# Two graph-attention layers on one core: TensorE in the source's order

## The chip, the cores and the metric

The kernel runs on one core of one Trainium2 chip, as one launch. The metric is the time of that launch in device microseconds. The version before takes 2741.27 us (median of three runs, 2739.28 to 2741.64 us).

A core has five engines with a queue each. In this kernel TensorE (PE) does matrix products and transposes, VectorE (DVE) and ScalarE (ACT) do elementwise work and reductions, GpSimd (POOL) issues the gathers and scatters (indirect DMAs), and SyncE (SP) issues the plain DMAs.

## What is computed

The inputs are `x`, 8 batches of 2048 nodes with 256 features, and `adj`, a 2048 x 2048 adjacency matrix of few ones (some 0.8% of its entries, and the diagonal). There are two layers, and each is followed by a residual and a layernorm over the features:

```python
# layer 0
h1, h2, h3 = x @ W1, x @ W2, x @ W3
e = leaky_relu(h1 @ h2.T, 0.2);  e = where(adj > 0, e, -1e12)
x = layernorm(x + relu(softmax(e) @ h3))
# layer 1, 4 heads of 64
q = x @ W;  e = leaky_relu(e_src[i] + e_dst[j]) where adj > 0   # per head
x = layernorm(x + elu(softmax(e) @ q))
```

Here `e_src` and `e_dst` are the products of `q` with the two halves of the vector `a`, per head. Only the neighbours of a node enter its softmax, so the kernel never forms a full 2048 x 2048 score matrix.

## The kernel before

**Units and slots.** The nodes are sorted by degree and cut into 16 tiles of 128. A tile t has `SLOTS[t]` slots, from 12 to 38, 301 in all: slot k of a tile is, for each of its 128 nodes, the k-th neighbour. A *unit* is one layer, one half of the batch (4 of 8 batches) and one tile. There are 64 units: layer 0 first half, layer 0 second half (both from the tile with 12 slots to the one with 38), then the two halves of layer 1. A unit with 38 slots is done in two parts of 19.

**What one unit of layer 0 does.** `before0` gathers the unit's own rows `xo`, copies them to a residual buffer `xr`, transposes them on TensorE (`transposed`, two stages with a copy by ScalarE after each), and multiplies by A = W1 W2^T (`projected`, two stages) to get `g`. For each slot GpSimd gathers the 128 neighbour rows into a ring of 16 buffers of two slots (`chunk_job`). `logits0` has VectorE form the products of the rows with `g`, four instructions per slot, and then a softmax over the slots. `sums0` has ScalarE scale each slot's rows by their weights, four instructions, and TensorE add the slot to an accumulator in PSUM by a product with an identity (`add_slot`); then the ring buffer is free. `after0` takes the finished sum `hs`: it transposes it, multiplies it by W3, adds the residual on VectorE, normalises on VectorE and ScalarE, stores the row to `x1s`, transposes it again, and makes the rows `q` of layer 1 with their attention terms `so` in four more products. The rows `q` are scattered to a table by GpSimd eight steps later.

**Layer 1.** `logits1` needs one small addition per slot and head, `sums1` multiplies by the weights on VectorE (four chunks of five) or ScalarE (the fifth), and TensorE adds as before. `after1` does the elu, the residual and the layernorm, and scatters the result. For the tile with 38 slots the two parts are combined first (`shares` gives their factors, with small products on TensorE).

**What sets the order.** All of this is written as Python generators, and a driver, `tick` (L928), advances them: one call is a *step*. A step issues gathers while ring buffers are free (`pump`), up to two slots of scores, and up to two `yield`s of the work at the head of each of three queues: `starts` (`before0`, `before1`), `ends` (`after0`, `after1`) and `lists` (the extraction of each tile's neighbours, done with VectorE in the first half of layer 0). Between two steps one slot's sum is issued. A start is queued when half of the unit three places earlier is summed (L961). A unit's sums don't begin while more than one end is still open (L950).

The program order that comes out is binding for GpSimd alone: `tc.manual_schedule(engines={mybir.EngineType.Pool})` (L339). For the other engines a planner reorders the instructions with its own model of their times, and the engines then run their queues in the planned order.

**Buffers.** Four PSUM banks (`ps`) serve transposes and projections in turn and four (`psa`) the accumulators. `g` has two buffers, `xo` two, `xr` three, `wide` four (for `xT`, `hT`, `y`, `x1T`), and `q` one.

Of the kernel before, what the change touches and what calls it, by code (L numbers as in the profile page):

```python
# [38 lines left out]
RING = 16  # L39
LEAD = 5  # L40
LATE = 6

SHARE = 5

# [81 lines left out]
def fast_path(  # L126
# [59 lines left out]
    def wide_tile(name):  # L186
        return wp.tile([P, 2 * QW], F32, tag="t", name=name)
# [148 lines left out]
        nc.vector.tensor_copy(orderR[:, :, r], pr)  # L336
    nc.vector.scalar_tensor_tensor(orderP, orderR, 2.0, half, ALU.mult, ALU.add)
    setup.__exit__(None, None, None)
    ctx.enter_context(tc.manual_schedule(engines={mybir.EngineType.Pool}))  # L339

    def checks():

# [51 lines left out]
    def normalise(dst, y, b, rstd, nmr):  # L394
# [2 lines left out]
            bias=nmr[:, b : b + 1], scale=rstd[:, b : b + 1],  # L397
        )

    def transposed(src, name, dst):  # L400

        for i in range(2):
            pt = ps_tile(f"ps_t_{name}_{i}")
            for j in range(4):
                nc.tensor.transpose(pt[:, ts(j, P)], src[:, ts(4 * i + j, P)], ident)  # L405
            yield
            nc.scalar.copy(dst[:, ts(i, 512)], pt)  # L407
        yield

    def projected(srcT, weight, name, evict):  # L410
        for i in range(2):
            pp = ps_tile(f"ps_p_{name}_{i}")
            for j in range(2):
                for k in range(KC):
                    nc.tensor.matmul(  # L415
                        pp[:, ts(j, C)],
                        lhsT=srcT[:, ts((2 * i + j) * KC + k, P)],
                        rhs=weight[:, k, :],
                        start=(k == 0),
                        stop=(k == KC - 1),  # L420
                    )
            yield
            evict(i, pp)
        yield

    class Unit:
        def __init__(self, layer, h, t):
# [78 lines left out]
    def before0(u):  # L506
        xo = xop.tile([P, HC], F32, tag="xo", name=f"xo_{u.name}")
        gather(xo, xg[u.h][:, :], order[:, u.t : u.t + 1])
        u.xr = xrp.tile([P, 2, HW], F32, tag="xr", name=f"xr_{u.name}")
        for r in range(2):  # L510
            for c in range(2):
                nc.sync.dma_start(
                    u.xr[64 * c : 64 * c + 64, r, :], xo[64 * r : 64 * r + 64, ts(c, HW)]
                )
        for _ in range(4):
            yield
        xT = wide_tile(f"xT_{u.name}")
# [144 lines left out]
    def after0(u):  # L662
        h, t, n = u.h, u.t, u.name
        while evictions:
            evictions.popleft()()
        hs = u.hs
        hT = wide_tile(f"hT_{n}")
        yield from transposed(hs, f"h_{n}", hT)
        y = wide_tile(f"y0_{n}")[:, :HC]

        def residual(i, pp):
            nc.vector.scalar_tensor_tensor(
                y[:, ts(i, 512)], pp, 0.0, u.xr[:, i, :], ALU.max, ALU.add
            )

        yield from projected(hT, w.w3, f"h_{n}", residual)
        yb = y.rearrange("p (b c) -> p b c", b=HB)
        mv = yield from statistics(yb, n)
        yield
        yield  # L680
        rstd, nmr = factors(mv, n)
        yield
        for b in range(HB):
            normalise(yb, yb, b, rstd, nmr)
            if b % 2 == 1:
                yield
        nc.sync.dma_start(x1s[h][ts(t, P), :], y)
        x1T = wide_tile(f"x1T_{n}")
        yield from transposed(y, f"x1_{n}", x1T)
        qrow = qp.tile([P, 2, QW], F32, tag="q", name=f"q_{n}")  # L690
        so = sp.tile([P, 2, HG // 2], F32, tag="so", name=f"so_{n}", bufs=2)
        for i in range(HB):
            r, j = divmod(i, 2)
            pq = ps_tile(f"ps_q_{n}_{i}")
            for k in range(KC):
                nc.tensor.matmul(  # L696
                    pq[:, : C + 2 * H],
                    lhsT=x1T[:, ts(i * KC + k, P)],
                    rhs=w.wqs[:, k, :],
                    start=(k == 0),  # L700
                    stop=(k == KC - 1),
                )
            yield
            nc.scalar.copy(qrow[:, r, ts(j, CD)], pq[:, :CD])
            nc.vector.tensor_copy(so[:, r, ts(j, H)], pq[:, CD : CD + H])  # L705
        for c in range(2):
            nc.sync.dma_start(
                own_d[h][ts(t, P), ts(c, HG // 2)].rearrange("(r p) g -> p r g", r=2),
                so[64 * c : 64 * c + 64],
            )  # L710

        def store():
            for r in range(2):
                scatter(
                    f"q{h}",
                    qg[h].rearrange("n (q c) -> (n q) c", q=2),
                    orderP[:, t, r : r + 1],
                    qrow[:, r, :],
                )
            tabled[0] += 1  # L720

        late.append((clock[0] + 8, store))
# [62 lines left out]
    def sums1(u):  # L785
        u.xr = xrp.tile([P, 2, HW], F32, tag="xr", name=f"xr_{u.name}")
        nc.sync.dma_start(u.xr.rearrange("p r c -> p (r c)"), x1s[u.h][ts(u.t, P), :])
        while evictions:
            evictions.popleft()()
        u.accs = []  # L790
        for i, (k0, K) in enumerate(u.parts):
            while u.p[i] is None:
                yield 0
# [23 lines left out]
            for c in range(chunks):  # L817
# [5 lines left out]
                for s in range(n):  # L823
# [1 line left out]
                    if s == n - 1:  # L825
                        credits[0] += 1
                    yield 1
            u.accs.append(acc)

    def after1(u):  # L830
        h, t, n = u.h, u.t, u.name
        v = u.accs[0]
        if len(u.accs) == 2:
            fs = shares(u, HG)
            v = wide_tile(f"v_{n}")[:, :HC]
            v = [v[:, ts(r, HW)] for r in range(2)]
            v2 = wide_tile(f"v2_{n}")[:, :HC]
            for r in range(2):
                for i, d in ((0, v[r]), (1, v2[:, ts(r, HW)])):
                    nc.vector.tensor_tensor(  # L840
                        d.rearrange("p (a d) -> p a d", d=D),
                        u.accs[i][r].rearrange("p (a d) -> p a d", d=D),
                        fs[:, i, r, :].unsqueeze(2).to_broadcast([P, HG // 2, D]),
                        ALU.mult,
                    )
                nc.vector.tensor_tensor(v[r], v[r], v2[:, ts(r, HW)], ALU.add)
            yield

        ex = wide_tile(f"ex_{n}")[:, :HC]
        for r in range(2):  # L850
# [89 lines left out]

    for t in up[:3]:
# [324 lines left out]
```

## Time and profile before

| | |
|---|---|
| median of the runs | 2741.27 us |
| the profiled execution | 2741.96 us |
| its span, first to last instruction | 2740.1 us |
| TensorE busy, matmuls | 1857.8 us, 68% of the span |
| TensorE busy, weight loads | 792.3 us, 29% |
| VectorE busy | 2270.1 us, 83% |
| ScalarE busy | 1827.9 us, 67% |
| GpSimd busy | 1515.4 us, 55% |
| granted TensorE clock, mean | 0.842 |
| moved by DMA | 749.51 MB, 274 GB/s in the mean |

"Busy" counts the instructions themselves and no waiting; an engine's idle time before an instruction is listed with what ended it. A mean over the span hides that the stages differ: the setup takes until some 200 us, layer 0 until some 1720 us, layer 1 the rest. A score instruction on VectorE takes 424 ns in the mean and its readout 82 ns, a scaling on ScalarE 506 ns from start to end (consecutive ones start 0.4 us apart), a product of a slot's sum 653 ns with eight of them in flight together.

### The profile page before, as it was taken

The page shows a single profiled execution, that of the slowest core. Times are in us where ns is not written, and L with a number is a line of the kernel's source. Part 1 is how long each engine was busy: PE and PEld are TensorE (multiplying, and loading weights), DVE is VectorE, ACT ScalarE, POOL GpSimd, SP SyncE. Part 2 cuts the span into 40 slices and gives each one's busy share as a digit, 9 for nine tenths or more (in the row PEclk, how much of TensorE's full clock was granted, in tenths as well). Part 3 has the DMA queues.
Part 4 walks back from the last instruction along what each step waited for, and adds up shares of the span by engine and source line. Part 5 has one row for each costly group of instructions (what it writes and reads, how often), then busy time and mean ns, then how long its engine had stood idle before and what let it go on. Part 6 is the DMA issues. An engine that isn't in the chain of part 4 may idle for free. (4 is left out here: it accounts for less than half of the span.)

```text
span 2740.1 us, 42566 instructions
## 1 busy us (share of the span) xinstructions
PE 1857.8 (68%) x12003; PEld 792.3 (29%) x12003; DVE 2270.1 (83%) x7247; ACT 1827.9 (67%) x4937; POOL 1515.4 (55%) x1506
## 2 busy tenths in 40 slices
PE   0148888888786866686878767756656667655763
PEld 0124434333332333343434323312221222211221
DVE  7679999999987876777787786788888888888996
ACT  6137787878879986867878779644445555554454
POOL 1353454545444544544454545577767777777773
PEclk9569999999988988898988888877877878877876
DMA  9996776777765566767686774899789998997892
GB/s 388 380 376 207 270 262 245 260 245 263 261 221 200 183 215 215 252 212 268 219 277 217 242 263 154 287 332 357 268 315 354 348 344 317 358 351 269 305 354 89
DMA packets 248036, 749.51 MB, mean 274 GB/s; under 512 B 55712, under 2 KB 73248, under 8 KB 241648
## 3 DMA queue, kind: packets, MB, share of 16 engines
q0 software_dynamic: 192064, 644.32, 66.5%
q1 hardware_dynamic: 54464, 101.21, 10.4%
q8 instruction: 98, 1.61, 0.2%
q10 hardware_dynamic: 1264, 1.18, 0.1%
q14 instruction: 146, 1.20, 0.1%
HBM read 721.50 MB, written 84.48 MB: 294 GB/s over the span
## 5 line engine op out<-in xcount | busy, mean ns | idle before, releaser
L612 PE MATMUL acc<-s,ident 64*64 64x512 f32 x9632 | 1336.4, 653 | 469.0 <-issue 285.4
L543 DVE CUSTOM_DVE_ANT_0 j<-s,g 128x256 bf16<-128x256 f32 x2408 | 1019.9, 424 | 199.1 <-DMA s<-xg,idx 133.0
L191 POOL DMA_INDIRECT s<-xg,idx x602 | 632.4, 1051 | 771.7 <-ACT s L634 280.9
L634 ACT ACTIVATE s<-s,e 128x256 f32<-128x256 f32 x2408 | 1000.1, 506 | 28.3 <-DVE e L569 27.4
L191 POOL DMA_INDIRECT s<-qg,idx x602 | 614.8, 1021 | 233.4 <-issue 123.7
L612 PEld LDWEIGHTS acc<-s,ident 64*64 64x64 f32 x9632 | 391.1, 144 | 1211.5 <-issue 777.6
L813 DVE TENSOR_TENSOR s<-s,p 128x2048 f32<-128x2048 f32 (+1 forms) x262 | 577.5, 2222 | 0.0
L809 ACT ACTIVATE s<-s,e 128x64 f32<-128x64 f32 x1472 | 357.8, 335 | 47.1 <-DVE e L777 35.8
L543 DVE DVE_READ_ACCUMULATOR2_ANT e<- 128x1 f32 x2408 | 197.0, 82 | 0.0
L696 PE MATMUL ps_q<-wqs,x1T 128*128 128x264 f32 x512 | 147.7, 426 | 35.9 <-ACT x1T L407 25.1
L199 POOL DMA_INDIRECT out_dram<-o,oidx x128 | 130.2, 1017 | 71.5 <-ACT o L395 36.7
L405 PE MATMUL ps_t_x<-ident,xo 128*128 128x128 f32 x256 | 56.7, 365 | 162.7 <-DMA xo<-xg,order 162.6
L383 ACT ACTIVATE z<-mv,roots 128x4 f32<-128x4 f32 x64 | 19.0, 297 | 212.2 <-DVE mv L373 212.1
L747 DVE TENSOR_TENSOR e<-s,own 128x32 f32<-128x32 f32 (+1 forms) x312 | 56.9, 186 | 104.0 <-DMA s<-qg,idx 97.6
L415 PE MATMUL ps_p_g<-A,xT 128*128 128x256 f32 x512 | 129.4, 399 | 8.9 <-DVE so L705 5.2
L415 PE MATMUL ps_p_h<-w_sb,hT 128*128 128x256 f32 x512 | 127.8, 392 | 1.4 <-ACT hT L407 1.4
L696 PEld LDWEIGHTS ps_q<-wqs,x1T 128*128 128x128 f32 x512 | 100.8, 206 | 88.4 <-ACT x1T L407 32.8
L395 ACT ACTIVATE o<-xr,nmr,rstd 128x256 f32<-128x256 f32 x128 | 66.3, 589 | 76.9 <-DVE nmr L391 67.3
L415 PEld LDWEIGHTS ps_p_g<-A,xT 128*128 128x128 f32 x512 | 96.7, 196 | 53.2 <-ACT s L634 8.1
L763 ACT ACTIVATE e<-e 128x304 f32<-128x304 f32 (+11 forms) x34 | 14.9, 439 | 143.7 <-DVE e L762 143.7
L491 DVE MAX8 m<-nb 128x8 f32<-128x2048 f32 x44 | 100.5, 2286 | 11.9 <-DMA nb<-edges,order 11.7
L415 PEld LDWEIGHTS ps_p_h<-w_sb,hT 128*128 128x128 f32 x512 | 92.0, 189 | 63.3 <-issue 17.9
(130 smaller groups left out, 1486.2 us busy)
## 6 DMA issues: line engine op xcount, KB each, us to landing
adj<-in_adj_dram SPq DMA_DIRECT2D x16, 1024.0 KB, 8.9
edges<-adj SPq DMA_DIRECT2D x16, 1024.0 KB, 19.8
xr<-xo SPq DMA_DIRECT2D x128, 128.0 KB, 6.9
x1s<-y SPq DMA_DIRECT2D x32, 512.0 KB, 7.3
xr<-x1s SPq DMA_DIRECT2D x32, 512.0 KB, 6.9
s<-xg,idx POOLq DMA_INDIRECT x602
s<-qg,idx POOLq DMA_INDIRECT x602
xg<-in_x_dram SPq DMA_DIRECT2D x4, 2048.0 KB
```

Of the source, the lines that this page charges most:

```text
L191: nc.gpsimd.indirect_dma_start(out=dst, out_offset=None, in_=table, in_offset=AT(ap=index, axis=0), bounds_check=table.shape[0] - 1, oob_i ...
L199: ins = nc.gpsimd.indirect_dma_start(out=table, out_offset=AT(ap=index, axis=0), in_=src, in_offset=None)
L395: nc.scalar.activation(dst[:, b, :], y[:, b, :], AF.Identity, bias=nmr[:, b : b + 1], scale=rstd[:, b : b + 1],)
L415: nc.tensor.matmul(pp[:, ts(j, C)], lhsT=srcT[:, ts((2 * i + j) * KC + k, P)], rhs=weight[:, k, :], start=(k == 0), stop=(k == KC - 1),)
L491: nc.vector.max(m[:, ts(i, 8)], v)
L543: nc.vector.tensor_tensor_reduce(out=jt, in0=rows[:, s, ts(b, C)], in1=u.g[:, ts(b, C)], scale=1.0, scalar=0.0, op0=ALU.mult, op1=ALU.add, ...
L612: nc.tensor.matmul(acc[r][64 * c : 64 * c + 64, :], lhsT=ident[rr, rr], rhs=rows[rr, s, c * 2 * w_ : (c + 1) * 2 * w_].rearrange("p (j w) ...
L634: nc.scalar.activation(v, v, AF.Copy, scale=u.p[i][:, b, k : k + 1])
L696: nc.tensor.matmul(pq[:, : C + 2 * H], lhsT=x1T[:, ts(i * KC + k, P)], rhs=w.wqs[:, k, :], start=(k == 0), stop=(k == KC - 1),)
L747: nc.vector.tensor_tensor(e[:, c * CHUNK : c * CHUNK + ns, :].rearrange("p s (b g) -> p s b g", b=HB), rows[:, :ns, :].rearrange("p s (b w ...
L809: nc.scalar.activation(v[:, a, g, :], v[:, a, g, :], AF.Copy, scale=pv[:, a, g : g + 1])
L813: nc.vector.tensor_tensor(v, v, pv.unsqueeze(3).to_broadcast([P, n * HB, H, D]), ALU.mult)
```

## The change

TensorE is added to the engines that follow the source's order. So that this order is a sensible one, the source is rewritten around it:

- `pause(n)` waits until the driver has made n more steps. `transposed`, `projected` and the `q` products now issue a stage and its copy in the same step and take one step per stage; there are fixed distances of `GAP` = 2 steps after a pair of transposes and before the first ones of an end, of 4 steps before the transposes of the normalised rows, and of 8 steps between the gather of `xo` and its transposes.
- The statistics, their factors and the normalisation of an end follow each other without pauses.
- The driver advances the two oldest ends in each step, and the head alone of `starts` and of `lists`; a unit's sums wait only when more than two ends are open.
- In layer 1 the combination of two parts (`combine`) is put in the queue `evictions`, which is emptied ahead of the next unit's sums, where it stood in `after1`.

The instructions and their number stay the same.

```diff
+GAP = 2
...
-    ctx.enter_context(tc.manual_schedule(engines={mybir.EngineType.Pool}))
+    ctx.enter_context(
+        tc.manual_schedule(engines={mybir.EngineType.Pool, mybir.EngineType.PE})
+    )
...
+    def pause(steps):
+        then = clock[0] + steps
+        while clock[0] < then:
+            yield
+
     def transposed(src, name, dst):
         for i in range(2):
             pt = ps_tile(f"ps_t_{name}_{i}")
             for j in range(4):
                 nc.tensor.transpose(pt[:, ts(j, P)], src[:, ts(4 * i + j, P)], ident)
-            yield
             nc.scalar.copy(dst[:, ts(i, 512)], pt)
-        yield
+            yield from pause(1)
+        yield from pause(GAP)
...
-            yield
             evict(i, pp)
-        yield
+            yield from pause(1)
...
-        for _ in range(4):
-            yield
+        yield from pause(LATE + 2 if u.index else 2)
         xT = wide_tile(f"xT_{u.name}")
...
         hs = u.hs
+        yield from pause(GAP)
         hT = wide_tile(f"hT_{n}")
...
         mv = yield from statistics(yb, n)
-        yield
-        yield
         rstd, nmr = factors(mv, n)
-        yield
         for b in range(HB):
             normalise(yb, yb, b, rstd, nmr)
-            if b % 2 == 1:
-                yield
         nc.sync.dma_start(x1s[h][ts(t, P), :], y)
+        yield from pause(2 * GAP)
         x1T = wide_tile(f"x1T_{n}")
...
-            yield
             nc.scalar.copy(qrow[:, r, ts(j, CD)], pq[:, :CD])
             nc.vector.tensor_copy(so[:, r, ts(j, H)], pq[:, CD : CD + H])
+            yield from pause(1)
...
-            u.accs.append(acc)
-
-    def after1(u):
...
+            accs.append(acc)
+        u.v = accs[0]
+
+        def combine():
             fs = shares(u, HG)
...
+        if len(accs) == 2:
+            evictions.append(combine)
+
+    def after1(u):
+        h, t, n = u.h, u.t, u.name
+        while evictions:
+            evictions.popleft()()
+        v = u.v
...
         for queue in queues:
-            for _ in range(min(len(queue), 2)):
-                if queue and next(queue[0], queue) is queue:
-                    queue.popleft()
+
+            for work in list(queue)[: 2 if queue is ends else 1]:
+                for _ in range(2):
+                    if next(work, work) is work:
+                        queue.remove(work)
+                        break
         clock[0] += 1
...
-        while len(ends) > 1:
+        while len(ends) > 2:
             tick(0)
```

More of the change, by code (lines that the diff above doesn't have):

```diff
@@ L789, in sums1 @@
             evictions.popleft()()
-        u.accs = []
+        accs = []
         for i, (k0, K) in enumerate(u.parts):
@@ L827, in sums1 @@
                     yield 1
-            u.accs.append(acc)
-    def after1(u):
-        h, t, n = u.h, u.t, u.name
-        v = u.accs[0]
-        if len(u.accs) == 2:
+            accs.append(acc)
+        u.v = accs[0]
+        def combine():
             fs = shares(u, HG)
-            v = wide_tile(f"v_{n}")[:, :HC]
-            v = [v[:, ts(r, HW)] for r in range(2)]
-            v2 = wide_tile(f"v2_{n}")[:, :HC]
+            v = wide_tile(f"v_{u.name}")[:, :HC]
+            u.v = [v[:, ts(r, HW)] for r in range(2)]
+            v2 = wide_tile(f"v2_{u.name}")[:, :HC]
             for r in range(2):
-                for i, d in ((0, v[r]), (1, v2[:, ts(r, HW)])):
+                for i, d in ((0, u.v[r]), (1, v2[:, ts(r, HW)])):
                     nc.vector.tensor_tensor(
                         d.rearrange("p (a d) -> p a d", d=D),
-                        u.accs[i][r].rearrange("p (a d) -> p a d", d=D),
+                        accs[i][r].rearrange("p (a d) -> p a d", d=D),
                         fs[:, i, r, :].unsqueeze(2).to_broadcast([P, HG // 2, D]),
@@ L845, in after1 @@
                     )
-                nc.vector.tensor_tensor(v[r], v[r], v2[:, ts(r, HW)], ALU.add)
-            yield
+                nc.vector.tensor_tensor(u.v[r], u.v[r], v2[:, ts(r, HW)], ALU.add)
+        if len(accs) == 2:
[5 more added lines that the diff above has]
+        v = u.v
         ex = wide_tile(f"ex_{n}")[:, :HC]
```

## The prediction

> **What bounds the kernel now.** I read the page's busy shares first, then busy time by stage, then the waits of the longest stage, then one of its units in the timeline. No engine bounds the whole span (VectorE 83%), so I cut it by when a unit's last sum left TensorE (every slot is 8 `acc` matmuls): layer 0's first half of the batch ends at 960 us, its second half at 1719 us, layer 1 fills the rest. Each row: stretch and length; busy time and count on PE, weight load, DVE, ACT, POOL; clock, DMA share, GB/s.
>
> ```profile
> 205.00:505.00 300.00, 254.55 (x1356) 119.72 (x1352) 289.48 (x1149) 234.37 (x573) 138.23 (x133) 0.93 0.71 249
> 505.00:825.00 320.00, 264.77 (x1432) 114.37 (x1432) 302.47 (x1270) 250.28 (x620) 154.86 (x146) 0.92 0.73 246
> 825.00:960.00 135.00, 98.65 (x648) 42.55 (x640) 107.25 (x513) 125.47 (x314) 66.29 (x65) 0.86 0.58 194
> 960.00:1650.00 690.00, 510.58 (x3152) 249.05 (x3148) 522.92 (x2500) 545.55 (x1341) 323.65 (x309) 0.86 0.70 237
> 1720.00:2740.00 1020.00, 629.81 (x4888) 219.61 (x4888) 861.59 (x1368) 526.46 (x1805) 723.17 (x709) 0.80 0.85 309
> ```
>
> VectorE bounds 205 to 825 (96%, 95%); it also extracts the neighbour lists there. ScalarE bounds 825 to 960 (93%). In 960 to 1650 nothing passes 79%: that stage has room. Its waits on TensorE and VectorE (total us, times, longest):
>
> ```profile
> PE ps_t_x L405 <- DMA xo<-xg,order: 122.5, 13, 12.2
> ...
> DVE j L543 <- DMA s<-xg,idx: 112.0, 74, 7.2
> ```
>
> TensorE's 510.6 us of work and 122.5 us of waiting for a unit's own rows make 633 of the 690. One unit shows how (start, length, work, idle before it):
>
> ```profile
> 1103.91 7.10 PE L612 MATMUL acc<-s,ident 64*64 64x512 f32 x64
> 1122.30 1.09 PE L405 MATMUL ps_t_x<-ident,xo 128*128 128x128 f32 x4 [11.29 <-DMA xo<-xg,order]
> ```
> ```profile
> 1113.88 1.04 POOL L191 DMA_INDIRECT xo<-xg,order  x1 [0.30 <-issue]
> ...
> 1125.60 1.09 POOL L191 DMA_INDIRECT s<-xg,idx  x1 [5.12 <-PE acc L612]
> ```
>
> The planner placed the transposes of `xo` behind eight slots done in one burst; `xo` is only requested at 1113.88 and lands 8.4 us later. Meanwhile no sum runs, no ring buffer comes free, GpSimd stops gathering (5.12 us) and VectorE starves.
>
> **What the Trainium skill says.** "TensorE: Matmul & The Clock Gate", § Measured speedup vs the span model: matmuls start and end strictly in program order. The trace agrees: sums whose rows were scaled stand 11.29 us behind one transpose. "DMA: Bandwidth & Descriptors", § Anatomy of one DMA, prices a GpSimd-issued DMA at some 2 us plus bytes at 436 GB/s, 3.2 us for the 512 KB of `xo`; here it took 8.4 us behind other gathers, and that is what I use. "Perfetto Trace Analysis", § Optimization Strategy, advises looking for gaps regime by regime on the engine that binds; done above.
>
> **The change, part by part.** No instruction is added or dropped. TensorE's order becomes the source's, ScalarE, VectorE and SyncE stay with the planner. Positions below are driver steps (calls of `tick`), counted through the generators.
>
> *1. The wait for `xo` (gain).* `xo` is gathered eight steps ahead of its transposes, where it had two; its four `xr` copies on SP stay behind the gather as before. A step in this stage is some 2.3 us, so eight are 18 us against 8.4 us plus two gathers queued ahead (2 x 1.3). The wait goes. Sums come one per step, so buffers and gathers come evenly too. What is late next: ScalarE with 545.6 us, then VectorE with 522.9; TensorE's own work is 510.6. The best share a binding engine reaches here is 93 to 96% (rows above), but with other engines idle for 15% and more. Here VectorE is nearly as full, and ScalarE's queue holds copies of what TensorE makes one instruction earlier. Bounds: 82% (hardly better than now) and 95%. I take 88%: 545.6 / 0.88 = 620, gain 70 us; ends 665 (gain 25) and 574 (gain 116).
>
> *2. Stages spread and two units overlapped (nothing, with a bound).* Projections of a unit go from 10 steps after its end to 21. Work that hides it: the next unit's sums, 12 to 38 steps. VectorE's residual and statistics, ScalarE's normalisation, `x1s<-y` on SP come 5 to 6 steps later; the next reader of `x1s` is layer 1, hundreds of us on. The transposes of `y` have six steps (13 us) after the last projection; in the timeline around 1104 to 1115 that chain took 11. The one `q` buffer is tighter: the scatter goes out 29 steps after a unit's end, the next unit's `q` copies come K + 17 steps after it, 1 to 3 steps for K of 13 to 15, against 7 to 10 before. A landing of 8 us could hold ScalarE up to 5 us in ten units: 0 to 50 us, of which the half beside a fuller VectorE is free. I count it inside the 88%.
>
> *3. The queue of starts (loss).* Only the head of `starts` is driven, at one stage per step: a start takes 8 + 4 + 2 steps and the next begins one step on, so 15 per unit, where it took 5. The first units have 12 to 17 slots, so starts run just in time: g of units 2 to 8 gets its projection after slot 5, 5, 4, 4, 4, 3, 1 of the unit before; from unit 9 on it is early again. In source order TensorE cannot take it sooner. So VectorE, having scored unit n, waits for unit n's first sums before it can score n+1. Gap: weights of the softmax 3.0 us (from 376.1 to 379.1 in the timeline of VectorE), then 6, 6, 5, 5, 5, 4, 2 slots on ScalarE at 4 x 0.41 = 1.65 us, its copies between them some 3.5 us, last sum, projection and copy of g 3.0 us: 19.4, 19.4, 17.7, 17.7, 17.7, 16.1, 12.8, together 121 us. In the gap VectorE still does the lists (two or three MAX8 at 2.29 and one or two replacements at 2.28: 7 to 11 us). Then it scores: 112 slots at 4 x 0.467 = 1.87 us = 209 us, and 2.5 us of other work squeezed between them in each unit = 18 us. Sum 348 us. Counting scores in the timeline, these seven units took from 216.0 to 513.2, 297 us. Loss 51 us. Bounds: the gap 4 us shorter or longer in each unit: 23 to 79. Nothing gives it back: from unit 9 on VectorE is full as before.
>
> *4. `combine` ahead of the next unit's sums (nothing).* It runs for two units of layer 1. The next unit needs the accumulators it frees, before and after; the same 6 multiplications and adds of 0.69 us.
>
> *5. Layer 1.* TensorE has only sums there, in the order of the source already; DMA (85%) and VectorE bind. 0, bounds -8 and +8.
>
> Sum against the profiled run's own 2742.0 us: -70 + 51 + 0, rounded to -20: 2722; the median of the runs is 0.7 us less, so 2721.
>
> **The rivals.**
> *A. Slower: ScalarE's queue keeps waiting for TensorE.* Each unit of layer 0 has 10 copies and 4 q copies out of PSUM; the planner puts them into ScalarE's queue by its own clock. If TensorE is a microsecond behind it at each, ScalarE stays near today's 79 to 82%; the gain of part 1 shrinks to 25 us and part 3 decides: 2741 - 25 + 51 = 2767. The turning point is 545.6 / (690 - 51) = 85%. For it: in 960 to 1650 ScalarE waits already 42.6 us for the softmax and 27.4 us for statistics. Against: copies other than those of `xo` cost it only 26 us.
> *B. Much faster.* The lists and the residuals fill the gap of part 3 (loss 25) and ScalarE reaches 92% (593 us, gain 97): 2669. Against: 7 to 11 us of lists don't fill 17.
> *C. The wait for `xo` hides nothing.* Then the second half stays, 2741 + 51 = 2792. Against: 633 of 690 us.
> *D. No change*: parts 1 and 3 cancel, 2741.
>
> **How the numbers follow.** Forecast 0.44, A 0.32, B 0.10, C 0.05, D 0.09. 0.2% (5.5 us) is about what a measurement of this kernel tells from no change. Faster 0.54, same 0.09, slower 0.37. The forecast's own range is 2695 to 2736; with A and most of B it is 2660 to 2790.
>
> **What would show it.** Right: in the second half no wait of TensorE on `xo`, ScalarE at 88%, last sum of that half's units some 620 us after the first; in 205 to 530 us VectorE's share falls from 96 to about 83%, with waits on the g copy. Wrong: VectorE as full as before at the start (part 3), ScalarE below 85% with waits on PSUM copies or on the q scatter (part 1), or layer 1 different from 1020 us.

## The result, and the profile after

The changed kernel takes **2905.24 us** (median of four runs, 2901.32 to 2906.62) against 2741.45 us for the kernel before, measured beside it: a ratio of 1.059, interval 1.0566 to 1.0613. The forecast was 2721 us, with a range of its own from 2695 to 2736 and of 2660 to 2790 with the rivals. The profiled execution took 2901.32 us (its span is 2899.5 us), so it stands for the median.

The span is cut where a unit's last sum leaves TensorE, which is read from the trace of each kernel by counting `acc` matmuls, eight to a slot (us):

```
                            before    after
to the end of unit 0         205.2    201.4
units 1 to 8                 349.1    497.7   +148.6
units 9 to 15                405.8    398.6     -7.2
units 16 to 30               690.0    663.5    -26.5
unit 31                       68.9     66.7     -2.2
layer 1, first half          509.2    524.9    +15.7
layer 1, second half         483.9    520.1    +36.2
after the last sum            28.0     26.6     -1.4
```

With the 3.8 us gained by the end of unit 0 this adds up to the 159.4 us between the two spans. So three things happened: units 1 to 8 lost far more than the 51 us of part 3, units 16 to 30 gained far less than the 70 us of part 1, and layer 1, which was to stay as it is, lost 52 us. TensorE's granted clock was a little lower than before (0.821 against 0.842 in the mean), but its busy time did not grow (1853.6 us against 1857.8), so the lower clock is not what cost the time.

Busy time of the changed kernel by stage (stretch and length; PE, weight load, DVE, ACT, POOL; clock, DMA share, GB/s), in two answers:

```profile
201.00:699.00 498.00, 279.79 (x1589) 136.24 (x1585) 366.34 (x1421) 273.89 (x669) 163.44 (x157) 0.76 0.54 180
...
1097.00:1761.00 664.00, 528.10 (x3152) 245.35 (x3148) 524.03 (x2484) 538.51 (x1337) 322.30 (x306) 0.90 0.73 245
1828.00:2899.00 1071.00, 635.36 (x4880) 220.23 (x4880) 861.63 (x1366) 526.61 (x1808) 715.56 (x706) 0.80 0.82 293
```
```profile
205.00:530.00 325.00, 166.06 (x944) 80.81 (x944) 223.72 (x861) 165.56 (x406) 96.49 (x93) 0.73 0.50 168
```

VectorE, busy 96% of the first stretch before, is busy 223.72 of 325 us = 69% there now (83% was forecast). In the second half ScalarE is busy 538.51 of 664 us = 81% (88% was forecast, 79% before).

**Units 2 to 8.** From the last score of unit 1 to the last score of unit 8 the trace of the changed kernel has 415.9 us (230.5 to 646.4), where the prediction had 348 and the kernel before 297. Waits of the stretch, weight loads left out (what waits, for what; total us, times, longest):

```profile
PE acc L620 <- ACT s L642: 150.7, 7, 33.3
ACT e L571 <- DVE e L570: 131.6, 7, 30.9
...
DVE so L709 <- ACT q L708: 55.6, 10, 10.9
...
POOL nb L192 <- PE acc L620: 42.7, 2, 24.5
DVE j L551 <- ACT g L531: 36.5, 9, 7.8
```

VectorE, ScalarE and TensorE take turns: TensorE waits for scaled rows seven times, 21.5 us each on average (150.7 / 7), ScalarE as often for the weights. One gap, after unit 5, on VectorE and on GpSimd (start, length, work, idle before it):

```profile
463.22 0.23 DVE L577 TENSOR_TENSOR e<-e,s 128x64 f32<-128x64 f32 x1
474.33 0.16 DVE L709 COPY so<-ps_q 128x4 f32<-128x4 f32 x1 [10.88 <-ACT q L708]
478.47 0.43 DVE L551 CUSTOM_DVE_ANT_0 j<-s,g 128x256 bf16<-128x256 f32 x1 [3.98 <-ACT g L531]
...
479.45 2.30 DVE L500 MAX8 m<-nb 128x8 f32<-128x2048 f32 x1
```
```profile
470.46 0.98 POOL L192 DMA_INDIRECT s<-xg,idx  x1 [20.34 <-ACT s L642]
473.85 0.98 POOL L192 DMA_INDIRECT nb<-edges,order  x1 [2.41 <-ACT s L642]
```

The last score ends at 461.4 and the next starts at 478.47: 17.1 us, against 17.7 for this gap in the prediction. But the lists that were to run in it come after it. The list's gather needs a ring buffer, which the sums of this very gap free, so it goes out at 473.85; and on VectorE the copy of `so`, which waits for ScalarE's copy of `q`, and the first score stand in front. Over the seven gaps (124.5 us by the trace; 121 forecast) VectorE spends 9.1 us on lists. Of the 69.3 us of lists in the stretch, 60.2 run between scores.

**Units 16 to 30.** TensorE's largest waits there:

```profile
PE ps_t_x L415 <- ACT y L398: 50.1, 12, 7.1
PE ps_q L701 <- ACT x1T L416: 23.0, 6, 5.7
```

The wait for `xo` (122.5 us before) is gone; in a unit's timeline a slot's sums now stand between the stages (1200.22 below), where before eight or nine slots came in one burst, 14 times in these units (the longest burst is now six slots):

```profile
1197.28 1.09 PE L620 MATMUL acc<-s,ident 64*64 64x512 f32 x8
1198.30 1.99 PE L425 MATMUL ps_p_g<-A,xT 128*128 128x256 f32 x8
1200.22 1.09 PE L620 MATMUL acc<-s,ident 64*64 64x512 f32 x8
1201.24 1.99 PE L425 MATMUL ps_p_g<-A,xT 128*128 128x256 f32 x8
```

**Layer 1.** One wait grew on GpSimd and one on VectorE, the longest from 15.5 to 19.8 us and from 4.1 to 13.1 us. Layer 1 of the kernel before, then of the changed one:

```profile
POOL out_dram L199 <- ACT o L395: 36.7, 14, 15.5
...
DVE e L747 <- DMA s<-qg,idx: 91.7, 67, 4.1
```
```profile
POOL out_dram L200 <- ACT o L398: 76.9, 31, 19.8
...
DVE e L752 <- DMA s<-qg,idx: 144.7, 73, 13.1
```

How one makes the other, in the changed kernel on ScalarE, GpSimd and VectorE:

```profile
2394.39 2.08 ACT L398 ACTIVATE o<-xr,nmr,rstd 128x256 f32<-128x256 f32 x4 [8.64 <-DVE nmr L394]
```
```profile
2385.41 0.99 POOL L192 DMA_INDIRECT s<-qg,idx  x1 [0.30 <-issue]
2395.27 1.03 POOL L200 DMA_INDIRECT out_dram<-o,oidx  x1 [8.86 <-ACT o L398]
...
2400.41 1.05 POOL L192 DMA_INDIRECT s<-qg,idx  x1 [0.30 <-issue]
```
```profile
2394.27 0.19 DVE L752 TENSOR_TENSOR e<-s,own 128x32 f32<-128x32 f32 x1
2407.31 0.19 DVE L752 TENSOR_TENSOR e<-s,own 128x32 f32<-128x32 f32 x1 [12.85 <-DMA s<-qg,idx]
```

GpSimd comes to the scatter of `out` before ScalarE has made `o`. It stands still for 8.86 us, then issues four scatters, and the next gather goes out 14 us after the last one. VectorE runs dry for 12.85 us. In the source a lone end now gets two stages in a step where it got one, so this scatter stands five steps, or five gathers of one slot each, earlier in GpSimd's queue: counted in the traces, the first unit's comes behind 53 gathers of layer 1 instead of 58.

### The profile page after: what moved, and what is told of

The parts are those of the page before. It is cut to its first block, busy times and chain, and to the rows that moved or that the text cites. A ratio compares the mean times of both kernels' runs of the same rounds, so it can differ in the third digit from the quotient of the medians.

```text
span 2899.5 us, 42500 instructions
## 1 busy us (share of the span) xinstructions
PE 1853.6 (64%) x12003; PEld 782.8 (27%) x12003; DVE 2288.9 (79%) x7247; ACT 1821.1 (63%) x4937; POOL 1510.6 (52%) x1506
## 5 line engine op out<-in xcount | busy, mean ns | idle before, releaser
L620 PE MATMUL acc<-s,ident 64*64 64x512 f32 x9632 | 1313.5, 665 | 627.5 <-issue 323.9
L620 PEld LDWEIGHTS acc<-s,ident 64*64 64x64 f32 x9632 | 383.2, 146 | 1320.6 <-issue 824.3
L701 PE MATMUL ps_q<-wqs,x1T 128*128 128x264 f32 x512 | 167.3, 456 | 71.6 <-DVE so L709 32.9
L571 ACT ACTIVATE e<-e 128x76 f32<-128x76 f32 (+11 forms) x34 | 8.9, 261 | 255.9 <-DVE e L570 255.4
L415 PE MATMUL ps_t_x<-ident,y 128*128 128x128 f32 x256 | 61.7, 378 | 151.6 <-ACT y L398 151.2
L768 ACT ACTIVATE e<-e 128x304 f32<-128x304 f32 (+11 forms) x34 | 14.9, 438 | 169.1 <-DVE e L767 169.0
```

Of the source, the lines that this page charges most:

```text
L620: nc.tensor.matmul(acc[r][64 * c : 64 * c + 64, :], lhsT=ident[rr, rr], rhs=rows[rr, s, c * 2 * w_ : (c + 1) * 2 * w_].rearrange("p (j w) ...
L701: nc.tensor.matmul(pq[:, : C + 2 * H], lhsT=x1T[:, ts(i * KC + k, P)], rhs=w.wqs[:, k, :], start=(k == 0), stop=(k == KC - 1),)
```

## The experiments

The first four ran together, and the kernel before took 2845.64 us beside them; layer 1 was slower there (last section). Their times are compared with that, and their stages with each other where it can be. Beside the other runs the kernel before took 2739.24 to 2741.8 us in the median.

**Two starts at a time.** The changed kernel with

```diff
-            for work in list(queue)[: 2 if queue is ends else 1]:
+            for work in list(queue)[: 1 if queue is lists else 2]:
```

> The changed kernel with two starts driven per step in place of one; nothing else differs. Theory (the queue of starts holds the projections of g back, so that VectorE idles after each unit's scores while its lists wait for a ring buffer): g of unit n now comes after 8 slots of unit n-2 in place of 5 slots of unit n-1, the first half of layer 0 ends near 960 to 990 us in place of 1098, and the time falls from 2905 to 2750 to 2790; layer 1 stays at some 1070 us. Rival (TensorE in the source's order follows ScalarE too closely, whatever the starts do): no more than 30 us gained, 2875 or more.

2827.36 us, 0.9933 of before (0.9912 to 0.9955). Units 1 to 8 take 359 us, against 501 in the next run, which was measured beside it and has the late starts; the first half of layer 0 ends at 966.7 us, inside the theory's range, and units 16 to 30 keep their gain at 661. The queue of starts is the cause of the large loss, and with it gone the change is no loss there.

**The output scatter later.** The changed kernel with

```diff
-        late.append((clock[0] + LATE, lambda: store(o)))
+        late.append((clock[0] + LATE + 5, lambda: store(o)))
```

> The changed kernel with the scatter of layer 1's results requested five steps later, where it stood relative to the sums in the kernel before. Theory (GpSimd stops at a scatter whose rows aren't normalised yet, and the gathers stand behind it): layer 1 falls from 1072 to some 1020 us, 2905 to 2855. Rival (layer 1 is longer for TensorE's order or for the combination moved): 2895 to 2910, and GpSimd's waits for the rows go but the gathers don't come sooner.

2938.86 us, 1.0317 (1.0289 to 1.0345), with the late starts still in it. Its layer 1 took 556 + 526 = 1082 us where the two runs with the early scatter beside it took 571 + 540 and 568 + 543, both 1111 us. So 29 us there, less than the 52 expected, and yet all of the loss: the run with the distance of `xo` alone, whose layer 1 is that of the kernel before, took 1083 us in it.

**TensorE by the planner.** The changed kernel with only GpSimd in the order of the source:

```diff
-        tc.manual_schedule(engines={mybir.EngineType.Pool, mybir.EngineType.PE})
+        tc.manual_schedule(engines={mybir.EngineType.Pool})
```

> The changed kernel with TensorE given back to the planner; distances, queues and the combination stay as changed. If the source's order on TensorE is what turns the late starts into idle time, the planner can take the projections of g ahead of the sums they stand behind: the first half of layer 0 ends near 960 us again, layer 1 stays 50 us longer, 2770 to 2800 in all. If the distances alone cost the time, whoever orders TensorE: 2880 or more.

2863.15 us, 1.0059 (1.0034 to 1.0083). Units 1 to 8 take 385 us against 501 with the source's order: the planner moves late starts forward, and that is worth 116 us, though not all of the loss (359 us with two starts at a time). Units 16 to 30 take 664 and 665 us with the two orders. In those units every stage stands behind the same number of slots in both traces.

**The distance of `xo` alone.** The kernel before with

```diff
-        for _ in range(4):
+        then = clock[0] + (LATE + 2 if u.index else 2)
+        while clock[0] < then:
             yield
```

> The kernel before with one edit: the transposes of a unit's own rows stand eight steps behind the gather in place of four; TensorE stays with the planner. If the wait for these rows bounds the second half of layer 0 (step 1 of the prediction), it goes and that half (960 to 1650 us) shortens by 25 to 70 us: 2670 to 2716. If the wait hides another limit (rival C), within 8 us of 2741.

2829.55 us, 0.9931 (0.9909 to 0.9952). But units 16 to 30 take 686 us, 4 less than the kernel before in its own trace, though only 3.3 us of the wait for `xo` are left. (That trace is not from these runs. In two pairs of runs with one source of layer 0, that layer took 0.4 and 0.9% longer here, so the gain may be up to some 10 us; that is an estimate.) One of its units on TensorE:

```profile
1062.83 7.96 PE L613 MATMUL acc<-s,ident 64*64 64x512 f32 x72
...
1082.26 2.13 PE L697 MATMUL ps_q<-wqs,x1T 128*128 128x264 f32 x4 [6.97 <-ACT x1T L407]
1084.18 1.06 PE L405 MATMUL ps_t_x<-ident,xo 128*128 128x128 f32 x4
```

Nine slots in one burst, then another stage that isn't ready. What the wait for `xo` hid has come to the surface. What made this run faster as a whole isn't shown: there is no profile of the kernel before from these runs.

**Both repairs.** The two edits of the first two runs together.

> The changed kernel with two starts driven at a time (as in two_starts) and the output scatter of layer 1 put five steps later in GpSimd's order (as in late_out), so where it stood before the change. Theory (two separate costs, the queue of starts and the early scatter): the savings add. The run with two starts alone stood at 0.993 of the kernel before and had 571 + 540 = 1111 us for the two halves of layer 1; late_out had 1082. So layer 1 some 1082 us on a chip as slow as that one, layer 0 as in two_starts (second half's first fifteen units 661 us), and 0.993 - 29/2846 = 0.983 of the kernel before. Rival (the scatter's place is worth something only when layer 1 starts late or unevenly): 0.993.

2702.46 us, 0.9854 (0.9837 to 0.9871). Units 1 to 8 are back at 349 us, layer 1 at 508 + 486 = 994 us (993 before), and units 16 to 30 stay at 657. Of the 200.5 us between the profiled spans of this kernel and the changed one (2899.5 - 2699.0) 149 lie in units 1 to 8 and 51 in layer 1: the whole loss is these two.

**The early scatter alone.** The kernel before with

```diff
-        late.append((clock[0] + LATE, lambda: store(o)))
+        late.append((clock[0] + LATE - 5, lambda: store(o)))
```

> The kernel before with nothing changed but the output scatter of layer 1: five steps earlier in GpSimd's order (one step after the normalisation instead of six). Theory (the early scatter alone makes layer 1 slower, as GpSimd's queue stands still for a result that isn't ready): layer 0 as in the kernel before (ends at 960 and 1719 us), the two halves of layer 1 some 30 to 50 us longer, GpSimd's wait of the output scatter for ScalarE some 77 us instead of 37: 1.010 to 1.018 of the kernel before. Rival (it was something else in layer 1, such as the order of its sums on TensorE or of the combine): 1.000.

2802.08 us, 1.0211 (1.0192 to 1.023). Layer 0 is that of before; layer 1 takes 535 + 524 us, 65 more than before. The two waits of the changed kernel appear in it:

```profile
POOL out_dram L199 <- ACT o L395: 83.0, 33, 15.5
...
DVE e L747 <- DMA s<-qg,idx: 153.3, 74, 12.8
```

Five steps of one scatter's place cost 60 us here by the medians, more than the 52 us that layer 1 of the changed kernel lost.

**The lists ahead of unit 1.** The changed kernel with all neighbour lists gathered and extracted first:

```diff
-        if j == 0:
-            for t in up[:3]:
-                jobs.append((lambda: True, lambda t=t: list_job(t)))
-        elif j + 2 < NT:
-            t = up[j + 2]
-            jobs.append((lambda: True, lambda t=t: list_job(t)))
+        if j < 2:
+            for t in (up[:3], up[3:])[j]:
+                jobs.append((lambda: True, lambda t=t: list_job(t)))
...
-        if 0 < j and j + 2 < NT:
-            lists.append(neighbours(up[j + 2]))
+        if j == 0:
+            for t in up[3:]:
+                lists.append(neighbours(t))
```

> The changed kernel with the neighbour lists of all units gathered and extracted ahead of unit 1 instead of one at each unit. Its total gets no better by that, since some 38 MAX8 and 25 replacements of 2.3 us then stand ahead of unit 1 with nothing beside them. What counts is the stretch from the last score of unit 1 to the last score of unit 8: 416 us in the changed kernel. Theory (that stretch is the gap of 121 us plus 227 us of scores and small work, plus the lists, which don't fit into the gap since their gather waits for a buffer that only the sums in that gap free): 340 to 355 us. Rival (the lists did fill part of the gap, and something else stretched it): 385 us or more.

2930.82 us, 1.0683 (1.0665 to 1.0702), as the lists now stand bare in front. The stretch from the last score of unit 1 to that of unit 8 takes 366.5 us (324.9 to 691.4), between the two expectations and nearer the theory. The seven gaps in it sum to 121.2 us, the number of the prediction. Of the 68 us that the stretch was longer than predicted, 49 go with the lists. The rest is mostly a wait that the prediction had at nothing, and that the lists had covered in part: the second half of `g` comes one slot's sums after the first, so VectorE stops again after the first scores of a unit. Outside the gaps it waits 23.6 us for `g` here and 13.1 in the changed kernel (54.4 and 36.5 us with the waits that end a gap):

```profile
DVE so L709 <- ACT q L708: 55.8, 10, 10.9
DVE j L551 <- ACT g L531: 54.4, 14, 7.8
```

**The ends alone.** The kernel before with the changed kernel's `after0` of layer 0 (`pause`, the copies behind their matmuls) and its way of driving `ends`; starts, the distance of `xo` and TensorE's planner stay, and the scatter of `out` keeps its place:

```diff
+        yield from pause(GAP)
         hT = wide_tile(f"hT_{n}")
...
+        yield from pause(2 * GAP)
         x1T = wide_tile(f"x1T_{n}")
...
-        while len(ends) > 1:
+        while len(ends) > 2:
```

> The kernel before with the distances of the changed kernel between the stages of a unit's end alone, and two ends in progress: starts and the distance of xo as before, TensorE's order by the planner, the output scatter where it stood before. Theory (the 26 us that the second half of layer 0 gained come from the spread ends, since the distance of xo alone gave 4 us): from the last sum of unit 15 to that of unit 30 660 to 668 us, and with layer 1 unchanged 0.990 to 0.993 of the kernel before. Rival (the spread ends and the distance of xo are needed together): 680 to 690 us and 0.998 to 1.000.

2691.12 us, 0.981 (0.9794 to 0.9827): more than the changed kernel with both repairs, without touching TensorE's order or `xo`. Units 16 to 30 take 653 us. The busy times of that stretch, and then TensorE in one of its units:

```profile
955.00:1608.00 653.00, 522.71 (x3152) 246.65 (x3145) 523.47 (x2502) 540.78 (x1341) 325.01 (x309) 0.89 0.76 251
```
```profile
1089.45 1.16 PE L726 MATMUL ps_q<-wqs,x1T 128*128 128x264 f32 x4
1090.44 1.89 PE L449 MATMUL ps_p_h<-w_sb,hT 128*128 128x256 f32 x8
1092.27 1.09 PE L645 MATMUL acc<-s,ident 64*64 64x512 f32 x8
1093.28 1.99 PE L449 MATMUL ps_p_h<-w_sb,hT 128*128 128x256 f32 x8
1095.21 4.52 PE L645 MATMUL acc<-s,ident 64*64 64x512 f32 x40
```

ScalarE is at 540.78 of 653 us = 83%, and still nothing binds alone; but a slot's sums stand between most stages, and the burst that is left has five slots. The gain is beyond both expectations, and TensorE's wait for `xo` fell from 122.5 to 43.5 us although `xo` stands where it stood.

**Two ends, old distances.** The kernel before with the changed driving of `ends` only (two works, two stages of each in a step; the scatter of `out` kept in place).

```diff
+            if queue is ends:
+                for work in list(queue)[:2]:
+                    for _ in range(2):
+                        if next(work, work) is work:
+                            queue.remove(work)
+                            break
+                continue
...
-        while len(ends) > 1:
+        while len(ends) > 2:
```

> The kernel before with the changed kernel's way of driving the ends alone (two ends in progress, two stages of each in a step), without the distances between stages; the output scatter of layer 1 stays where it stood in GpSimd's order. Theory (the second half's gain comes from the distances, which put a slot's sums between any two groups of projections): the projections stand as close together as before or closer, so 685 us or more from the last sum of unit 15 to that of unit 30 (690 before, 653 with the distances), and 0.998 or more of the kernel before. Rival (it comes from two ends overlapping): 650 to 670 us and 0.980 to 0.990.

2755.67 us, 1.0049 (1.0033 to 1.0066); units 16 to 30 take 698 us. Two ends in progress give nothing if their stages follow each other in half the slots: TensorE then waits for what the stages read, 51.9 us for `y`, 24.5 for `xT`, 20.5 for `hs` and 14.9 for `hT` in units 16 to 30.

**Both repairs, TensorE by the planner.** As "both repairs", with the third run's edit.

> The changed kernel with both repairs (two starts at a time, output scatter five steps later), but TensorE's order by the planner again. Theory (TensorE's source order is worth nothing by itself; it only made the late starts dear): within 0.5% of the run with both repairs in the source's order, so 0.980 to 0.990 of the kernel before, the second half's first fifteen units 650 to 662 us. Rival (the source's order carries part of the gain): 0.991 or more.

2696.31 us, 0.9834 (0.9818 to 0.985), units 16 to 30 at 660 us: the same as in the source's order, within the intervals. With starts that aren't late, the edit that the change is named after makes no difference that these runs can tell; in units 16 to 30 every stage stands behind the same number of slots in the two traces.

**The scatter still later.** "The ends alone" with `LATE + 9` in place of `LATE + 5`.

> The kernel with spread ends alone (ends_alone, 0.981) with the output scatter of layer 1 another four steps later in GpSimd's order. In ends_alone GpSimd still waits 37 us, 13 times, with its queue at that scatter. Theory (each such wait holds the gathers behind it): the waits fall below 10 us, and layer 1's two halves (505 + 488 us) get 10 to 30 us shorter: 0.970 to 0.978. Rival (the waits that are left are covered by buffers already gathered): 993 us in the two halves and 0.981.

2684.02 us, 0.9787 (0.9771 to 0.9804). GpSimd's wait for the rows of `out` was to fall below 10 us; it went from 37.0 to 30.7 us, and layer 1 from 993 to 984. The interval overlaps that of the ends alone, so this is the lowest time of the study but not shown to be a step beyond it.

**No steps without a slot.** The kernel before stops adding slots, at the start of a unit, until only one end is in progress. Counted through the generators these are 29 steps in units 16 to 30. Here two ends may be in progress, one stage of each in a step:

```diff
+            if queue is ends:
+                for work in list(queue)[:2]:
+                    if next(work, work) is work:
+                        queue.remove(work)
+                continue
...
-        while len(ends) > 1:
+        while len(ends) > 2:
```

> The kernel before with one thing taken away: the steps in which the driver adds no slot because it waits until only one unit's end is in progress. Counted through the generators, these are 29 steps between the last slots of units 15 and 30, three or more in each of units 17 to 22 but one or none in 25 to 30, and in them the transposes and projections of the ending unit follow each other with no sums between. Here two ends may be in progress and each gets one stage in a step, as a lone one did before; no distance is added between stages, starts and the output scatter stay. Theory (those steps were what the second half lost; the wait for xo only stood where they would have shown): 650 to 665 us from the last sum of unit 15 to that of unit 30, 0.980 to 0.987 of the kernel before. Rival (the distances are needed as well): 675 to 690 us and 0.993 to 1.000.

2729.76 us, 0.9954 (0.9936 to 0.9971). Only its times are at hand, no profile. The theory falls: the stops are worth about a quarter of what the ends alone gave (0.46% of 1.9%).

**Copies right behind their matmuls.** As the last one, and in `after0` each copy out of PSUM stands ahead of the `yield` instead of behind it. For the transposes this comes to the following; the projections and the products of `q` are treated alike, and the starts keep the old form:

```diff
-            yield
             nc.scalar.copy(dst[:, ts(i, 512)], pt)
+            yield
```

> As no_stops (no steps without a slot, two ends in progress, one stage of each in a step; 0.995 of the kernel before), and besides each copy or residual out of PSUM in a unit's end stands in the source right behind the matmuls it reads, as in the changed kernel, instead of one step later. Theory (where the copy stands decides when ScalarE and VectorE hand the next stage its operand): 650 to 662 us from the last sum of unit 15 to that of unit 30, 0.980 to 0.986. Rival (the distances between stages do it): as no_stops, 0.993 to 0.997.

2735.39 us, 0.998 (0.9971 to 0.9989), units 16 to 30 at 680 us. It isn't the copies.

**Two steps more ahead of the transposes.** As "no steps without a slot", with nothing but distances added:

```diff
+        for _ in range(2):
+            yield
         hT = wide_tile(f"hT_{n}")
         yield from transposed(hs, f"h_{n}", hT)
+        yield
...
         yield from transposed(y, f"x1_{n}", x1T)
+        yield
```

> As no_stops, and besides two steps ahead of the transposes of hs and one more step between transposes and projections of a unit's end, the copies a step behind their matmuls as before. Theory (distances between stages do it, as TensorE then no longer meets the copies of hs and of the transposes too early): 650 to 662 us from the last sum of unit 15 to that of unit 30, 0.980 to 0.986. Rival (the place of the copies does it): as no_stops, 0.993 to 0.997.

2686.02 us, 0.98 (0.9782 to 0.9819), units 16 to 30 at 652 us. The distances carry it: from 0.9954 to 0.98 of the kernel before by four added steps. Where the stages stand, as slots behind the unit's last slot (read from the traces, mean of units 17 to 29), and what units 16 to 30 take:

```
                    transposes  projections  transposes  projections   us
                    of hs       of hT        of y        of x1T
before              0.6 to 1.6  3.6 to 4.6   13.6, 14.7  16.1 to 17.6  690
two ends, old       1.0 to 1.0  2.0 to 3.0    7.0, 8.0    9.0 to 10.0  698
copies near         1.0 to 2.0  4.0 to 5.0   14.0, 15.0  17.0 to 20.0  680
the ends alone      3.0 to 4.0  7.0 to 8.0   14.0, 15.0  18.0 to 21.0  653
two steps more      3.0 to 4.0  7.0 to 8.0   17.0, 18.0  21.0 to 24.0  652
```

The two fast rows share the first two columns. "Copies near" and "the ends alone" have almost the same last two, so the first stages of an end make the difference. How they do it is read from the traces and was not tried by itself. In copies-near a unit's last stages, the first ones of the next unit's end and a `g` come within some eight slots, and the other slots then go in one burst, at whose end something is late again (here `xo`, 92.6 us in units 16 to 30; the view names VectorE, but the rows of `xo`, requested at 1111.74, landed at 1120.1):

```profile
1105.64 1.16 PE L722 MATMUL ps_q<-wqs,x1T 128*128 128x264 f32 x4
1106.72 6.24 PE L638 MATMUL acc<-s,ident 64*64 64x512 f32 x56
1120.23 1.09 PE L405 MATMUL ps_t_x<-ident,xo 128*128 128x128 f32 x4 [7.27 <-DVE e L569]
```

Bursts of eight or nine slots come 14 times before, 11 times in copies-near, three times with two steps more and never in the ends alone. But "two ends, old" has only one long burst and is the slowest, as its stages stand too near to what they read. Which of the four added steps does most was not tried, nor the distances together with the stops.

## Why the prediction was wrong, point by point

The profiled execution took 2901 us where the sum gave 2722. Part 1 fell short by 44 us, part 3 by 98 in units 1 to 8, part 5 by 52, and the stretches that no part counts gave 15 back.

**Part 1, the wait for `xo` (gain 70, measured 26, and not from it).** The step that failed is "TensorE's 510.6 us of work and 122.5 us of waiting for a unit's own rows make 633 of the 690", read as if the wait could be taken out of the sum. TensorE had less work in this stage than ScalarE and VectorE, and these went on while it waited: in the 13 waits, 122.5 us, ScalarE was busy for 90.6 us (74%, against 79% over the stage) and VectorE for 91.9 us (75%, against 76%). All 16 DMA engines were busy in them (share 0.97 to 1.03, against 0.70 over the stage), which fits `xo` coming in behind the gathers that the burst had let out; this was not tried by itself. Nor does the time follow the wait. TensorE waited for `xo` 122.5 us where units 16 to 30 took 690 us, 3.3 us at 686 (the distance of `xo` alone), 16.4 at 698 (two ends, old), 92.6 at 680 (copies near) and 43.5 at 653 (the ends alone). The advice that the prediction cites from "Perfetto Trace Analysis" is to look for gaps on the engine one optimises for; it looked on TensorE, where ScalarE had the most work. (What it cites from the Trainium skill on the order of matmuls stands in § The mechanism of the page that it names, just ahead of the section given.) Nor was it the planner that put the transposes of `xo` behind a burst: counted through the generators, the source of the kernel before has every stage of units 16 to 30 within half a slot of where the trace has it. In this half the source's order on TensorE had nothing to mend; only the new distances moved anything. ScalarE at 88% was a value between two bounds with no work behind it; 81% is near the bound of "hardly better than now", and 664 us near the 665 worked out for that bound. `xo` also stood four steps ahead before, not two: the driver took as many stages of a queue's head in a step as the queue had works, up to two, and mostly it had one.

**Part 2, stages spread (nothing).** It was put at nothing, and this is where the second half's gain came from. The stages were counted as "10 steps after its end" before and 21 after; the traces have the last projections at 17.6 and 21 slots. What mattered was the first stages, which went from 0.6 to 3.0 and from 3.6 to 7.0 slots, and the prediction asked only what the move could cost. In units 16 to 30 the runs give 10 us to the steps without a slot (690 to 680, with the copies near) and 27 to 28 us to the distances (680 to 653 and 652).

**Part 3, the queue of starts (loss 51, measured 119 in its stretch, 149 in units 1 to 8).** The mechanism was right, and so was the sum of the gaps, 121 us forecast, 124.5 and 121.2 in two traces. Some of that is luck: singly the gaps took 9.9 to 21.2 us in the changed kernel, where 12.8 to 19.4 were forecast. "In the gap VectorE still does the lists" failed: 9 of 69 us run in it, as the lists' gather hangs on a buffer that this gap frees. The other 60 us run between the scores, and 49 of the missing 68 went away with the lists; most of the rest is the wait for the second half of `g`, which has no term in the sum. The figure of five steps for a start before was wrong as well (it took ten, for the same reason as `xo`), but does not enter the sum. The other 30 us of units 1 to 8 lie ahead of that stretch (its start is 14.5 us later) and behind it (unit 8 ends 52.7 us after its last score, 41.1 before), and part 3 didn't count them.

**Part 4, `combine`: nothing.** Never tried by itself. "Both repairs" has it, and its layer 1 took 994 us against 993.

**Part 5, layer 1 (nothing, within 8).** 52 us. The step that failed is "0, bounds -8 and +8". The prediction looked at TensorE, DMA and VectorE, and not at what the new way of driving `ends` does to GpSimd, which had been in the source's order all along: the scatter of `out` came five steps earlier. That move alone cost the kernel before 65 us in layer 1, and taking it back brought the changed kernel's to 994 us. The scatters of layer 0 were counted through, those of layer 1 were not.

**The rivals.** A's figure for the second half was the closest, 25 us of gain for 26.5 measured, but by luck, as its mechanism didn't come: ScalarE's waits for copies' inputs from TensorE fell, those for `xT` from 29.7 to 9.9 us. C was right that taking away the wait for `xo` gains next to nothing, but left the second half as it was, where the spread ends gained 26.5 us. None counted a loss in layer 1, and so none reached 2905; with 119 in place of 51 and 52 for layer 1, part 1 at 26 gives 2742 - 26 + 119 + 52 = 2887.

## What to carry to other kernels

When a driver issues work round by round, a stage's place counts on every engine that follows the source, and a change to how many stages a round takes moves them all: list for each in-order queue what now stands earlier, and ask whether its input is ready. A wait is not time to be gained by itself: first ask whether the engines with more work stand still during it, and what would be ready if it were gone. When filler work is to cover a gap, follow its own inputs back: if the same gap releases them, it covers nothing.

## What the runs showed of the hardware

The same kernel, the one before, took 2739 to 2742 us beside most runs and 2845.64 us beside the first four, 3.8% more. Its granted clock was not lower there (0.850 to 0.856, elsewhere 0.840 to 0.851). Most of the difference is in layer 1. The run with the distance of `xo` alone has layer 1 of the kernel before, and took 1083 us in it against 993; the later scatter and "both repairs" share a source of layer 1, 1082 and 994 us (9% more in both pairs). Of layer 0 the changed kernel and the later scatter share the source, 1827.9 and 1835.9 us (0.4% more), and so do "both repairs" and two starts at a time, 1678.2 and 1693.9 us (0.9% more).

In the traces of these four runs GpSimd waits with its gathers for releasers that the profile doesn't show, 72 to 92 us in 45 to 59 waits (85.4 us in layer 1 of the run with the later scatter); in no other trace of this study does it. What they are was not looked into. Whether it was another chip isn't known either: the next four runs, half an hour later, bear the same chip number, and beside them the kernel before took 2741.80 us.
